# A fused convolution, attention and expert kernel: step places by kind of slot, and all places set anew

## The chip, the cores and the metric

The kernel runs on one core of one Trainium2 chip. The metric is the device time of one execution in microseconds (us), the median over several runs. TensorE is called PE here, VectorE DVE, ScalarE ACT, GpSimd POOL, and SyncE SP. SP issues most of the DMAs. POOL issues the indirect ones (scatters of rows, and adds into the output).

## The reference

The input `x` is 8 images of 56x56 places with 256 channels, in float32, so 25,088 tokens. Cut to what matters:

```python
# layer 0: 32 narrow paths, each 1x1 to 4 channels, 3x3, 1x1 back to 256, with batch norms
paths = vmap(_path)(x, W1, ..., W2, ..., W3, ...)
x = relu(paths.sum(axis=0) + x)
# layer 1, on tokens t of 256 channels
y = _ln_t(t)                                   # attention of 8 heads with 32 channels
kv = einsum('bhnd,bhne->bhde', ln(y), ln(y)) / N          # one matrix for each image
t = t + (einsum('bhnd,bhde->bhne', y, kv) + y)
z = _ln_t(t)                                   # experts: 8, the best 2 for each token
out = z
for e in range(8):
    out = out + combine[:, e:e+1] * (gelu(z @ w1[e] + b1[e]) @ w2[e] + b2[e])
t = t + out
```

Attention needs the sum `kv` over a whole image before it can treat that image's first token, and an expert's tile of rows needs the routing of tokens from many places.

## The kernel before

**Chunks and slots.** An image is cut into 7 chunks of 448 tokens, so there are 56 chunks. The main loop runs over 65 slots. In slot s, the third convolution of chunk s is computed (16 steps of `pair`, two pairs each, and 8 of `sum_paths`), beside the first convolution of chunk s+2, the second one of chunk s+1, the end of chunk s-1 (`end_steps`: transposes, norms per head, and the products that go into `kv`), and the attention of chunk a = s-8. If a is the first chunk of an image, the slot also makes that image's matrix (`image_steps`). From slot 56 on there is no third convolution; this is called the tail here.

**Routing, plans, tiles.** Two chunks at a time are routed (`route_steps`), and their rows scattered by POOL into `regions` by expert. After some chunks (`closing`) a plan of tiles is made (`plan_steps`): which 256 rows of which expert each tile takes. A tile is worked on in five steps (`moe_steps`): `tile_in` (transposes `te`, L1404), two `tile_mid` (products `ph`, L1448, ACT Gelu), and two `tile_out` (products `py`, L1464 and L1468, ACT scaling into `y`), after which POOL adds `y` into the output (L1486). The same steps start the load of later tiles' rows (L1383, 259 KB) and weights (L1393, 513 KB) on SP. There are 210 tiles; slots 19 to 55 have three or four each, and 36 are left after slot 64.

**The order.** PE, DVE and ACT run in the order in which the program emits instructions. The order is not planned: each step has a place between 0 and 1 in its slot, and `issue` sorts the slot's steps by place. The places of `pair` and `sum_paths` follow from weights, and are spread over the slot; those of the other steps come from lists in `places`. A group with a begin and an end (`"tiles"`, `"route"`, `"plan"`) is spread between the two. POOL and SP are not in that order: the framework's scheduler orders them.

**Lists and slots.** Slots 0 to 7 have lists `"... alone"`. The others share one list for each group of steps, with exceptions for the attention of an image's first chunk, for the tail, and for `end_steps` in slots 8 to 20. `"tiles"` holds two begins:

```python
work_of.append((places["tiles"][s <= known_in[r]], places["tiles"][2], moe_steps(upto, goal)))
```

In the first slot in which a new plan is known (`s <= known_in[r]`), tiles begin at the second value, else at the first. These slots are called first slots here: 18, 21, 25, 28, 32, 35, 39, 42, 46, 49, 53, 56 and, in the tail, 59, 60, 62 and 64.

**Kinds of slots.** By a modulo 7, with slots 21 to 55: 0 makes an image's matrix (22, 29, 36, 43, 50); 1 routes one chunk and makes a plan; 2 routes two chunks (24, 31, 38, 45, 52); 3 is a first slot without routing (25, 32, 39, 46, 53); 4 routes two and makes a plan; 5 has no routing (27, 34, 41, 48, 55); 6 is a first slot which routes two (21, 28, 35, 42, 49). So 6 does the work of 2, and 3 nearly that of 5 (5 also scatters the second chunk of the group before).

Of the kernel before, what the change touches and what calls it, by code (L numbers as in the profile page):

```python
# [25 lines left out]
def kernel(  # L26
# [38 lines left out]
    NCH = N // CH  # L65
    NG = P // 32
    NJ = NP // NG
    S = B * NCH
    A = NCH + 1
# [26 lines left out]
    taps = ctx.enter_context(tc.tile_pool(name="taps", bufs=1))  # L96
# [160 lines left out]
    def is_chunk(s):  # L257
        return 0 <= s < S
# [115 lines left out]
    own = setup.tile([P, P // 16, 16], F32, name="own")  # L374
# [229 lines left out]
    def unordered(ins, group, keep=()):  # L604
# [7 lines left out]


    places = {
        "after": [7, 5, 5, 3, 6, 5, 6, 5, 10],
        "attention": [0.108, 0.235, 0.378, 0.514, 0.579, 0.689, 0.744, 0.798, 0.881, 0.94],
        "attention first": [0.396, 0.487, 0.578, 0.669, 0.742, 0.953, 0.99, 0.99, 0.99, 0.99],
        "attention last": [
            0.19, 0.311, 0.432, 0.553, 0.65, 0.65, 0.65,
            0.693, 0.741, 0.778, 0.802, 0.938, 0.938, 0.938,  # L620
        ],
        "attention first last": [
            0.611, 0.692, 0.774, 0.856, 0.921, 0.962, 0.982,
            0.982, 0.982, 0.982, 0.982, 0.982, 0.982, 0.982,
        ],
        "conv1": [0, 0, 0.111],
        "conv1 alone": [0, 0.003, 0.016],
        "conv2": [0.621, 0.658, 0.658, 0.675],
        "conv2 alone": [0.531, 0.629, 0.629, 0.806],
        "end": [0.109, 0.151, 0.244, 0.244, 0.337, 0.431, 0.551, 0.681, 0.761, 0.908],  # L630
        "end first": [0.109, 0.151, 0.244, 0.244, 0.337, 0.431, 0.551, 0.741, 0.771, 0.92],
        "end alone": [0.121, 0.156, 0.166, 0.226, 0.306, 0.386, 0.386, 0.636, 0.73, 0.865],
        "fetch": [0.103],
        "image": [
            0.001, 0.028, 0.054, 0.081, 0.115, 0.134,
            0.161, 0.187, 0.214, 0.241, 0.267, 0.294,
        ],
        "tiles": [0.029, 0.205, 0.99],
        "conv3": [0.7, 0.9],
        "plan": [0.64, 0.983],  # L640
        "route": [0.005, 0.373],
        "route last": [0, 0.002],
        "scatter": [0.302, 0.46],
        "scatter last": [0.35],
        "taps": [0.124],
        "taps alone": [0.413],
    }

    unit, sums = {}, {}
# [916 lines left out]
    def put_off(m):  # L1566

        return m % NCH == NCH - 1 and m + 1 + A < S

    known_in = [  # L1570
        m + A + 1 + (1 if m >= S - NCH else 2) + (1 if put_off(m) else 0) for m in closing
    ]
    r, upto = -1, -2
    waiting, left = [], []
    for s in range(S + A + 1):
        a = s - A
        work_of = []
        era = " alone" if s < A else ""
        if s <= S:
            work_of.append((0.0, 1.0 if is_chunk(s) else 0.1, conv3_steps(s)))  # L1580
        if is_chunk(s + 2):
            work_of.extend(at("conv1" + era, conv1_steps(s + 2)))
        if is_chunk(s + 1):
            work_of.extend(at("taps" + era, [(0.0, lambda: spread_taps(s + 1))]))
            work_of.extend(at("conv2" + era, conv2_steps(s + 1)))
        if is_chunk(s - 1):
            if s < S:
                few = " first" if A <= s < known_in[1] else era
                work_of.extend(at("end" + few, end_steps(s - 1)))
            else:  # L1590
                work_of.append((0.12, 0.99, end_steps(s - 1)))
        if is_chunk(a + 1):
            work_of.extend(at("fetch", [(0.0, lambda: fetch(a + 1))]))
        if is_chunk(a):
            opens = a % NCH == 0
            if opens:
                work_of.extend(at("image", image_steps(a // NCH)))
            if a + A > S:
                work_of.extend(at("attention first last" if opens else "attention last", attn_steps(a)))
            else:  # L1600
                work_of.extend(at("attention first" if opens else "attention", attn_steps(a)))
        work_of.extend(left)
        left = []
        group = waiting
        if waiting and put_off(waiting[0]):
            group = [] if waiting[0] == a - 1 else waiting[:1]
        if group and (len(group) == 2 or group[-1] % NCH == NCH - 1):
            last_image = group[-1] >= S - NCH
            compute, scatters = route_steps(group)
            rt = places["route" if s < S else "route last"]  # L1610
            work_of.append((rt[0], rt[1], compute))
            if last_image:
                work_of.append((places["scatter last"][0], 0.995, sum(scatters, [])))
            else:
                work_of.append((places["scatter"][0], 0.995, scatters[0]))
                left = [(0.0, places["scatter"][1], steps) for steps in scatters[1:]]
            if group[-1] in closing:
                work_of.append((places["plan"][0], places["plan"][1], plan_steps(closing.index(group[-1]))))
            waiting = waiting[len(group) :]
        while r + 1 < len(closing) and known_in[r + 1] <= s:  # L1620
            r += 1
        if r >= 0 and r + 1 < len(closing):
# [3 lines left out]
            work_of.append((places["tiles"][s <= known_in[r]], places["tiles"][2], moe_steps(upto, goal)))  # L1626
# [71 lines left out]
```

## Time and profile before

| what | value |
|---|---|
| median of 3 runs (lowest, highest) | 3053.82 us (3053.51, 3058.21) |
| time of the profiled execution | 3075.17 us |
| span of the profiled execution | 3072.7 us |
| PE busy, matmuls | 2850.7 us, 16901 |
| DVE, ACT, POOL busy | 2143.9, 1923.6, 1801.4 us |
| mean granted PE clock | 0.966 |
| bytes moved by DMA | 538.19 MB |

The profiled execution was 21 us longer than the median run, 0.7%. Busy times are sums of the profile's records; matmuls are pipelined and their ends are modelled, so PE can be called busy while it waits a little. A slot's bounds in the trace are taken from DVE operations on line 669: each of slots 0 to 55 has 32 of them, and a slot is the time from its first to the first of the next.

### The profile page before, as it was taken

To read this page: it belongs to the slowest core of one execution; us is meant where nothing else is said; L and a number is where in the kernel's file an instruction comes from. 1 tells how busy PE (TensorE), PEld (TensorE's weight loads), DVE (VectorE), ACT (ScalarE), POOL (GpSimd) and SP (SyncE) were. 2 spreads that over 40 slices of the span, in tenths; PEclk is the share of its full clock that TensorE was granted. 3 is DMA by queue.
4 is the path that set the end of the run, shared out by engine and by line. 5 is a ranking of instruction groups with operands and counts; after the bars stand their busy time and mean duration, and the time that the engine had idled before them with its cause. 6 is when DMAs were issued, how large, how long until landed. Compare 5 with 4: busy or idle time off the path is not lost.

```text
span 3072.7 us, 54357 instructions
## 1 busy us (share of the span) xinstructions
PE 2850.7 (93%) x16901; PEld 1656.5 (54%) x16901; DVE 2143.9 (70%) x5705; ACT 1923.6 (63%) x3859; POOL 1801.4 (59%) x1333
## 2 busy tenths in 40 slices
PE   7999989899999999999999999999999997887898
PEld 3334444444555555555555555555555554776787
DVE  6777888888878777787777787777778783543100
ACT  4666666556666666666766766666666663444455
POOL 2332254545566765666766766576664555677677
PEclk9999899999999999999999999999999998988899
DMA  3655454447577777777777776788887766998897
GB/s 102 146 118 131 111 149 138 135 111 189 146 180 164 216 168 201 176 182 211 188 193 178 194 205 160 198 193 177 201 171 184 182 172 136 235 246 212 211 225 172
DMA packets 373233, 538.19 MB, mean 175 GB/s; under 512 B 91488, under 2 KB 283344, under 8 KB 372944
## 3 DMA queue, kind: packets, MB, share of 16 engines
q1 hardware_dynamic: 289984, 430.49, 49.9%
q0 software_dynamic: 82368, 103.47, 20.4%
q8 instruction: 135, 2.21, 0.3%
q14 instruction: 154, 1.26, 0.2%
q10 hardware_dynamic: 592, 0.76, 0.1%
HBM read 248.42 MB, written 192.75 MB: 144 GB/s over the span
## 4 chain that ended last, share of the span: by engine, by line
PE 43%; DVE 4%; issue 3%; ACT 3%; POOL 2%; DMA 1%; another core or an unknown queue 1%; POOLq 0%; ACTq 0%; DVEq 0%; SPq 0%
PE ph L1448 10%; PE py L1468 8%; PE c L661 7%; PE su L682 6%; PE te L1404 2%; PE py L1464 2%; PE at L1011 2%; PE c L324 2%; PE kv L838 2%; DVE r L669 1%; ACT r L666 1%; DMA out_dram<-y,index 1%; POOL hsd L802 1%; PE at L1007 1%
## 5 line engine op out<-in xcount | busy, mean ns | idle before, releaser
L669 DVE SCALAR_TENSOR_TENSOR r<-c,nb,r 128x448 f32<-128x448 f32 x1792 | 1126.8, 676 | 370.3 <-ACT r L666 325.2
L666 ACT ACTIVATE r<-c,b3t 128x448 f32<-128x448 f32 x1792 | 1039.0, 635 | 320.0 <-PE c L661 302.4
L661 PE MATMUL c<-hl,W3hl 64*128 64x448 f32 x3584 | 705.8, 428 | 39.9 <-ACT r L666 20.0
L1192 POOL DMA_INDIRECT regions<-pay,rrowi x448 | 429.9, 960 | 290.7 <-PE c L661 162.6
L661 PEld LDWEIGHTS c<-hl,W3hl 64*128 64x128 f32 x3584 | 333.8, 187 | 493.4 <-issue 221.5
L1486 POOL DMA_INDIRECT out_dram<-y,rows x258 | 408.2, 1582 | 323.2 <-ACT y L1472 248.5
L682 PE MATMUL su<-r,gather 128*32 128x448 f32 x3584 | 534.2, 567 | 16.4 <-DVE xT L688 9.2
L1448 PE MATMUL ph<-eT,w 128*128 128x256 f32 x1680 | 460.2, 405 | 35.4 <-ACT hT L1452 13.6
L1472 ACT ACTIVATE y<-py,rows 128x256 f32<-128x256 f32 x420 | 197.4, 474 | 428.3 <-PE py L1468 309.5
L1468 PE MATMUL py<-w,hT 128*128 128x256 f32 x1680 | 432.5, 382 | 1.5 <-issue 1.5
L1448 PEld LDWEIGHTS ph<-eT,w 128*128 128x128 f32 x1680 | 301.8, 196 | 169.1 <-issue 51.7
L802 POOL TENSOR_TENSOR hsd<-hsd,half 112x36 f32<-112x36 f32 x49 | 302.3, 6170 | 101.6 <-DVE hsd L800 101.6
L755 POOL TENSOR_TENSOR norm<-t,hmean 112x512 f32<-112x512 f32 x112 | 115.7, 1060 | 360.7 <-DVE hmean L744 191.6
L1452 ACT ACTIVATE hT<-ph,w 128x256 f32<-128x256 f32 x420 | 198.0, 478 | 196.0 <-PE ph L1448 107.4
L1486 POOL DMA_INDIRECT out_dram<-y,index x162 | 251.1, 1550 | 101.3 <-ACT y L1472 32.7
L1468 PEld LDWEIGHTS py<-w,hT 128*128 128x128 f32 x1680 | 291.3, 191 | 29.2 <-issue 2.3
L682 PEld LDWEIGHTS su<-r,gather 128*32 128x32 f32 x3584 | 99.5, 109 | 199.9 <-issue 98.3
L1464 PE MATMUL py<-b2hl,own 128*128 128x256 f32 x420 | 175.7, 418 | 9.2 <-issue 4.9
L1016 DVE SCALAR_TENSOR_TENSOR X<-at,rs,X 112x256 f32<-112x256 f32 x224 | 106.7, 476 | 105.5 <-PE at L1011 59.3
L324 PE MATMUL c<-R,W2t 96*32 96x448 f32 x1344 | 151.5, 553 | 2.5 <-ACT r L666 2.5
L1464 PEld LDWEIGHTS py<-b2hl,own 128*128 128x128 f32 x420 | 79.9, 190 | 136.7 <-issue 61.5
L1011 PE MATMUL at<-tab,tT 128*112 128x144 f32 x896 | 151.6, 293 | 0.1
(267 smaller groups left out, 3271.7 us busy)
## 6 DMA issues: line engine op xcount, KB each, us to landing
w<-Wd SPq DMA_DIRECT2D x210, 513.0 KB
rows<-regions SPq DMA_DIRECT2D x210, 259.0 KB
xi<-in_x_dram SPq DMA_DIRECT2D x56, 448.0 KB
hl<-hi SPq DMA_DIRECT2D x112, 224.0 KB
tTs<-xT SPq DMA_DIRECT2D x56, 448.0 KB
ts<-t SPq DMA_DIRECT2D x56, 448.0 KB
tT<-tTs SPq DMA_DIRECT2D x56, 448.0 KB
X<-ts SPq DMA_DIRECT2D x56, 448.0 KB
```

Of the source, the lines that this page charges most:

```text
L324: nc.tensor.matmul(ps[0][32 * g : 32 * g + 32, :CH], W2t[:, g, dy, :], R[:, g, :].rearrange("q (r w) -> q r w", w=W58)[:, dy : dy + ROWS, ...
L661: product = nc.tensor.matmul(tiles[g][:, :CH], W3hl[rows, ab, cg, :], hl[rows, ab, :], start=True, stop=True)
L666: nc.scalar.activation(r, tiles[0][:, :CH], AF.Relu, bias=b3t[:, cg, 2 * ab : 2 * ab + 1])
L669: nc.vector.scalar_tensor_tensor(r, tiles[1][:, :CH], nb3[:, cg, 2 * ab + 1 : 2 * ab + 2], r, op0=ALU.max, op1=ALU.add,)
L682: nc.tensor.matmul(ps[32 * c4 : 32 * c4 + 32, :CH], gather, unit.pop((s, 4 * u + c4)), start=(ab == 0), stop=(ab == NQ - 1),)
L802: nc.gpsimd.tensor_tensor(sd, sd, half[:T, :].rearrange("q (k h) -> q k h", k=KT), ALU.pow)
L1011: nc.tensor.matmul(ps[:, f * P : f * P + WT], tT[:, f, k * T : (k + 1) * T], tab[:, f, :], start=False, stop=(f == NF - 1),)
L1192: ins = nc.gpsimd.indirect_dma_start(out=regions[n], out_offset=bass.IndirectOffsetOnAxis(ap=v["row_i"][:, (m - group[0]) * KT + k, n : n ...
L1448: nc.tensor.matmul(ps, w[:, f * C + hf * P : f * C + (hf + 1) * P], eT[:, f, :], start=(f == 0), stop=(f == NF - 1),)
L1464: nc.tensor.matmul(ps, own.to_broadcast([P, P]), b2hl, start=True, stop=False)
L1468: nc.tensor.matmul(ps, hT[:, f, h * P : (h + 1) * P], w[:, (NF + f) * C : (NF + f + 1) * C], start=False, stop=(f == NF - 1),)
L1486: ins = nc.gpsimd.indirect_dma_start(out=out_rows, out_offset=at, in_=y[:, h, :], in_offset=None, compute_op=ALU.add, **partial,).ins
```

## The change

The main loop gets a name for the slot's kind (`era`): `" few"` for slots 8 to 20, `" image"` for slots that make an image's matrix, `" plan"` for those that make a plan; slots 54 and later have none. The lists of attention, both convolutions, taps, end, route and tiles exist once for each kind, and all values were chosen anew.

```diff
     places = {
-        "after": [7, 5, 5, 3, 6, 5, 6, 5, 10],
+        "after": [7, 5, 5, 4, 7, 4, 6, 4, 10],
         "attention": [0.108, 0.235, 0.378, 0.514, 0.579, 0.689, 0.744, 0.798, 0.881, 0.94],
+        "attention few": [0.128, 0.255, 0.398, 0.534, 0.599, 0.709, 0.764, 0.818, 0.901, 0.96],
...
-        "conv2": [0.621, 0.658, 0.658, 0.675],
+        "conv2": [0.621, 0.658, 0.675, 0.675],
+        "conv2 image": [0.556, 0.618, 0.618, 0.635],
+        "conv2 plan": [0.621, 0.658, 0.658, 0.675],
...
-        "end": [0.109, 0.151, 0.244, 0.244, 0.337, 0.431, 0.551, 0.681, 0.761, 0.908],
+        "end": [0.109, 0.151, 0.244, 0.244, 0.337, 0.431, 0.551, 0.681, 0.761, 0.887],
+        "end image": [0.109, 0.201, 0.244, 0.244, 0.337, 0.431, 0.551, 0.686, 0.761, 0.995],
+        "end plan": [0.109, 0.151, 0.244, 0.244, 0.337, 0.431, 0.551, 0.681, 0.761, 0.908],
-        "image": [
-            0.001, 0.028, 0.054, 0.081, 0.115, 0.134,
-            0.161, 0.187, 0.214, 0.241, 0.267, 0.294,
-        ],
-        "tiles": [0.029, 0.205, 0.99],
-        "plan": [0.64, 0.983],
+        "image": [0, 0.023, 0.049, 0.076, 0.085, 0.129, 0.156, 0.182, 0.209, 0.236, 0.247, 0.247],
+        "plan": [0.64, 0.994],
+        "tiles": [0.038, 0.044, 0.986],
+        "tiles image": [0.029, 0.106, 0.99],
+        "tiles plan": [0.029, 0.106, 0.99],
...
-        era = " alone" if s < A else ""
+        few = A <= s < known_in[1]
+        era = " alone" if s < A else " few" if few else " image" if a % NCH == 0 else ""
+        plans = [m + A + (2 if put_off(m) else 1) for m in closing]
+        if not era and s in plans:
+            era = " plan"
+        if s >= S - 2:
+            era = ""
```

The lists of the tail (`"attention last"`, `"attention first last"`) move by some hundredths. `"after"` gives how many tiles slots 56 to 64 take: slots 59 and 60 take one more, 61 and 63 one fewer.

In the order of PE, DVE and ACT this comes to the following. No step is added or dropped. Slots 0 to 7 and the plan slots 23, 26, 37, 44, 47 and 51 keep their order. In first slots 21 to 53, the tiles of the slot begin two or three pair steps earlier and are spread more widely; the order of slot 42 is then that of slot 45, and the order of slot 53 that of slot 48, but for a step here and there that passes its neighbour. In ordinary slots `products` (L838) goes ahead of one `pair` step. In image slots `values` of the first half goes ahead of one `pair` step, `centered` follows `mean` at once, the second convolution comes one `pair` step earlier, and `products` goes to the end of the slot. In slots 9 to 20, `attend` 2 and 3 go behind the next `pair` step. In the tail's first slots, tiles begin ahead of the attention instead of behind its first one or two steps. On POOL, 1086 of 1338 instructions keep their place in the order; where the tail's scatters run, up to four adds go ahead of a burst of them, and the longest run of scatters without an add becomes 11 (it was 14) in slot 56 and 8 (it was 6) in slots 57, 59, 61 and 63.

More of the change, by code (lines that the diff above doesn't have):

```diff
@@ L614 @@
     places = {
-        "after": [7, 5, 5, 3, 6, 5, 6, 5, 10],
+        "after": [7, 5, 5, 4, 7, 4, 6, 4, 10],
         "attention": [0.108, 0.235, 0.378, 0.514, 0.579, 0.689, 0.744, 0.798, 0.881, 0.94],
-        "attention first": [0.396, 0.487, 0.578, 0.669, 0.742, 0.953, 0.99, 0.99, 0.99, 0.99],
+        "attention few": [0.128, 0.255, 0.398, 0.534, 0.599, 0.709, 0.764, 0.818, 0.901, 0.96],
+        "attention first": [0.396, 0.487, 0.578, 0.669, 0.742, 0.953, 0.989, 0.989, 0.989, 0.989],
+        "attention first last": [
+            0.616, 0.697, 0.779, 0.861, 0.921, 0.921, 0.921, 0.939, 0.939, 0.939, 0.939, 0.939,
+            0.939, 0.955,
+        ],
@@ L618 @@
         "attention last": [
-            0.19, 0.311, 0.432, 0.553, 0.65, 0.65, 0.65,
-            0.693, 0.741, 0.778, 0.802, 0.938, 0.938, 0.938,
-        ],
-        "attention first last": [
-            0.611, 0.692, 0.774, 0.856, 0.921, 0.962, 0.982,
-            0.982, 0.982, 0.982, 0.982, 0.982, 0.982, 0.982,
-        ],
+            0.175, 0.296, 0.417, 0.538, 0.635, 0.635, 0.635, 0.678, 0.726, 0.763, 0.787, 0.923,
+            0.923, 0.923,
+        ],
+        "attention plan": [0.108, 0.235, 0.378, 0.514, 0.579, 0.689, 0.744, 0.798, 0.881, 0.94],
@@ L626 @@
         "conv1": [0, 0, 0.111],
-        "conv1 alone": [0, 0.003, 0.016],
-        "conv2": [0.621, 0.658, 0.658, 0.675],
-        "conv2 alone": [0.531, 0.629, 0.629, 0.806],
-        "end": [0.109, 0.151, 0.244, 0.244, 0.337, 0.431, 0.551, 0.681, 0.761, 0.908],
-        "end first": [0.109, 0.151, 0.244, 0.244, 0.337, 0.431, 0.551, 0.741, 0.771, 0.92],
-        "end alone": [0.121, 0.156, 0.166, 0.226, 0.306, 0.386, 0.386, 0.636, 0.73, 0.865],
-        "fetch": [0.103],
-        "image": [
-            0.001, 0.028, 0.054, 0.081, 0.115, 0.134,
-            0.161, 0.187, 0.214, 0.241, 0.267, 0.294,
-        ],
@@ L638 @@
-        "tiles": [0.029, 0.205, 0.99],
-        "conv3": [0.7, 0.9],
-        "plan": [0.64, 0.983],
+        "conv1 alone": [0, 0, 0.014],
+        "conv1 few": [0, 0, 0.111],
+        "conv1 image": [0, 0, 0.111],
+        "conv1 plan": [0, 0, 0.111],
+        "conv2": [0.621, 0.658, 0.675, 0.675],
+        "conv2 alone": [0.531, 0.629, 0.629, 0.806],
+        "conv2 few": [0.621, 0.658, 0.658, 0.675],
+        "conv2 image": [0.556, 0.618, 0.618, 0.635],
+        "conv2 plan": [0.621, 0.658, 0.658, 0.675],
@@ new lines @@
+        "conv3": [0.7, 0.9],
+        "end": [0.109, 0.151, 0.244, 0.244, 0.337, 0.431, 0.551, 0.681, 0.761, 0.887],
+        "end alone": [0.116, 0.151, 0.161, 0.221, 0.301, 0.379, 0.381, 0.631, 0.725, 0.86],
+        "end few": [0.109, 0.148, 0.244, 0.244, 0.337, 0.431, 0.551, 0.741, 0.771, 0.92],
+        "end image": [0.109, 0.201, 0.244, 0.244, 0.337, 0.431, 0.551, 0.686, 0.761, 0.995],
+        "end plan": [0.109, 0.151, 0.244, 0.244, 0.337, 0.431, 0.551, 0.681, 0.761, 0.908],
+        "fetch": [0.103],
@@ L641 @@
+        "image": [0, 0.023, 0.049, 0.076, 0.085, 0.129, 0.156, 0.182, 0.209, 0.236, 0.247, 0.247],
+        "plan": [0.64, 0.994],
         "route": [0.005, 0.373],
+        "route image": [0.005, 0.373],
         "route last": [0, 0.002],
+        "route plan": [0.005, 0.373],
         "scatter": [0.302, 0.46],
@@ L646 @@
         "taps alone": [0.413],
+        "taps few": [0.124],
+        "taps image": [0.114],
+        "taps plan": [0.124],
+        "tiles": [0.038, 0.044, 0.986],
+        "tiles image": [0.029, 0.106, 0.99],
+        "tiles plan": [0.029, 0.106, 0.99],
     }
@@ L1587 @@
             if s < S:
-                few = " first" if A <= s < known_in[1] else era
-                work_of.extend(at("end" + few, end_steps(s - 1)))
+                work_of.extend(at("end" + era, end_steps(s - 1)))
             else:
@@ L1600 @@
             else:
-                work_of.extend(at("attention first" if opens else "attention", attn_steps(a)))
+                name = "attention" + (" first" if opens else era)
+                work_of.extend(at(name, attn_steps(a)))
         work_of.extend(left)
@@ L1609 @@
             compute, scatters = route_steps(group)
-            rt = places["route" if s < S else "route last"]
+            own = era if era in (" plan", " image") else ""
+            rt = places["route" + own if s < S else "route last"]
             work_of.append((rt[0], rt[1], compute))
@@ L1625 @@
                 goal = min(known_after[r] - 2, goal if s < known_in[1] else tiles_by(s))
-            work_of.append((places["tiles"][s <= known_in[r]], places["tiles"][2], moe_steps(upto, goal)))
+            own = era if era in (" plan", " image") else ""
+            mine = places["tiles" + own]
+            work_of.append((mine[s <= known_in[r]], mine[2], moe_steps(upto, goal)))
             upto = goal
```

## Prediction, made before the run

> **What bounds it now.** I read the page's busy times first, then its slices of time.
>
> ```profile
> span 3072.7 us, 54357 instructions
> ...
> PE 2850.7 (93%) x16901; PEld 1656.5 (54%) x16901; DVE 2143.9 (70%) x5705; ACT 1923.6 (63%) x3859; POOL 1801.4 (59%) x1333
> ...
> PE   7999989899999999999999999999999997887898
> ...
> PEclk9999899999999999999999999999999998988899
> ```
>
> PE is the bound, at 93%. 222 us of the span are left idle by it. The middle is full; the dents are in the sixth and eighth slices (384 to 461 and 538 to 614 us, slots 9 to 15, no tiles yet) and from the 34th on (the tail). No step is added or dropped, so what can change is idle time, and time in which PE runs at a low clock.
>
> Next I cut the trace at slot bounds and asked for each engine's busy time by stretch. Columns: bounds, length, then busy time (count) of PE, PEld, DVE, ACT, POOL, then granted clock, DMA share, GB/s.
>
> ```profile
> 309.20:358.30 49.10, 44.33 (x237) 20.89 (x235) 37.35 (x93) 25.50 (x50) 12.52 (x7) 0.83 0.37 96
> ...
> 1151.60:1199.50 47.90, 47.87 (x300) 27.06 (x292) 31.29 (x67) 34.22 (x70) 34.39 (x24) 1.00 0.79 201
> ...
> 1728.60:1773.80 45.20, 44.96 (x278) 25.29 (x278) 31.18 (x66) 31.97 (x65) 32.77 (x23) 1.00 0.75 202
> ...
> 1823.30:1868.20 44.90, 44.68 (x282) 24.43 (x282) 31.29 (x68) 31.91 (x65) 32.23 (x22) 1.00 0.86 209
> 1868.20:1916.30 48.10, 46.15 (x289) 26.21 (x286) 36.95 (x101) 32.11 (x66) 28.59 (x20) 1.00 0.61 164
> ...
> 2017.20:2062.90 45.70, 45.24 (x294) 25.18 (x286) 36.41 (x98) 32.00 (x66) 29.21 (x21) 1.00 0.80 187
> 2062.90:2112.80 49.90, 48.85 (x300) 27.87 (x300) 31.35 (x66) 34.23 (x70) 35.89 (x25) 1.00 0.88 204
> ```
>
> These are slots 8, 27, 39, 41, 42, 45 and 46. Slot 42 (a first slot, three tiles) does the work of slot 45 (three tiles, also routing two chunks), but takes 48.1 us against 45.7; slot 46 (a first slot, four tiles) takes 49.9 against 47.9 of slot 27.
>
> The timeline of PE shows why; behind the arrow stands what ended the idle time in the bracket. In slot 42:
>
> ```profile
> 1872.51 0.46 PE L661 MATMUL c<-hl,W3hl 64*128 64x448 f32 x1 [0.46 <-DVE r L669]
> 1872.90 0.65 PE L729 MATMUL tu<-ident,xT 128*112 128x128 f32 x4
> 1873.48 0.96 PE L682 MATMUL su<-r,gather 128*32 128x448 f32 x8
> 1874.37 0.66 PE L1404 MATMUL te<-ident,rows 128*128 128x128 f32 x4
> ...
> 1879.06 0.22 PE L1146 MATMUL rk<-rboth,earlier 112*112 112x128 bf16 x1 [0.53 <-ACT r L666]
> ```
>
> Until the first `te` there is no tile work, so PE waits for DVE and ACT to free the buffers of `pair`; afterwards three tiles crowd into the rest.
>
> **First slots, the main term.** After the change, the order in slot 42 is that of slot 45, so a first slot should take as long as its ordinary twin has taken. From the stretches:
> - a modulo 7 = 6, three tiles: 47.9, 47.8, 47.8 and 48.1 us (slots 21, 28, 35, 42) against a mean of 46.0 (46.4, 46.0, 45.7 of slots 31, 38, 45): 1.9 x 4 = 7.5. Four tiles: 51.6 (slot 49) against 49.3 (slots 24 and 52, 48.9 and 49.7): 2.3.
> - a modulo 7 = 3, three tiles: 45.8, 45.8, 45.2, 44.9 (slots 25, 32, 39, 53) against 44.7 (44.9, 44.9, 44.3 of slots 34, 41, 48): 1.1 + 1.1 + 0.5 + 0.2 = 2.9. Four tiles: 49.9 (slot 46) against 47.9 (slot 27): 2.0.
>
> Together 14.7 us. The part that is plain idle time of PE (1.95 in slot 42 against 0.46 in slot 45, and so on) is 11.3; I take 14.7 and keep 8 as the low end. Slot 18 only starts loads: nothing. The earlier steps also issue row and weight loads on SP, where a new plan's first load waits for all scatters of its round, with `xi`, `tTs` and the output's base rows queued behind. In slot 42 that load is at 1878.62, and the round's last scatter at 1843.33: 35 us of cover, of which the move takes about 5. Without it, PE would wait by whatever the load is late beyond the two tiles by which rows are loaded ahead.
>
> **Ordinary slots.** `products` passes one `pair` step, 0.68 us of PE (L661 x4 above). Its input is POOL's `scale`. In slots 31, 38 and 45 the first product starts 0.06 us before the second `scale` ends; in slots 10, 12, 14 and 17, where PE waits for it, 0.95 before. So 0.89 us are free: nothing, or up to 0.5 in each of seven slots if POOL is later too. Tiles begin 0.009 of a slot later; such slots leave PE idle for 0.2 to 0.8 us, so over some 20 slots I bound this by -4 and +4. I take +1 for both.
>
> **Plan and image slots.** Plan slots keep their order, but for neighbours: nothing. In image slots DVE runs without pause up to the matrix's last part. Slot 29 shows what PE waits for:
>
> ```profile
> 1254.15 0.46 PE L914 MATMUL cs<-tab,mean_of 128*128 128x128 f32 x2 [0.35 <-issue]
> ...
> 1255.62 0.49 PE L914 MATMUL cs<-tab,mean_of 128*128 128x128 f32 x2 [0.90 <-issue]
> ```
>
> `values` of the first half ahead of two L669 operations (1.27 us together) brings the first `cs` forward, not the second, which waits for all of DVE's queue either way. Their sum stays near 1.25 us: nothing. PE idles 2.7 us in slot 29 (51.4 less 48.7 busy); what is left beside the 1.25 bounds a gain by 1.5, and I take as much for a loss: 7 us either way in five slots.
>
> **Few tiles.** In slot 9, DVE runs without pause from 364.61 to 379.71, and PE waits 0.45 and 0.52 us ahead of `attend` 2 and 3. Which of DVE's operations comes first inside this stretch does not move its end: nothing, and at most 1 us a slot either way, 9 in all.
>
> **Tail.** It has 79 us of PE's idle time (512 less 433 busy, from 2560), most of it beside bursts of scatters:
>
> ```profile
> 2698.52 1.12 PE L1404 MATMUL te<-ident,rows 128*128 128x128 f32 x4 [2.07 <-issue]
> 2702.97 2.08 PE L1448 MATMUL ph<-eT,w 128*128 128x256 f32 x4 [3.33 <-issue]
> 2708.51 2.07 PE L1448 MATMUL ph<-eT,w 128*128 128x256 f32 x4 [3.46 <-issue]
> 2712.76 0.58 PE L1464 MATMUL py<-b2hl,own 128*128 128x256 f32 x1 [2.18 <-issue]
> ```
>
> POOL issues 16 scatters between 2685 and 2711. PE loses 11.0 us in these four waits, and at a clock of 0.79 over 2680 to 2720 another 8.4: 19.4 us for a burst. Slots 56, 61 and 63 show the like. The change mixes adds and scatters anew but takes away none, and no wait there names an add or a place. I take nothing, with one burst, 19.4, as the bound either way.
>
> **The sum.** -14.7 + 1 = -14 us. The profiled execution would go from 3075.2 to 3061, the median from 3053.8 to 3040 (the profile's own time stays 21 us above).
>
> **Rivals.**
> - *No net change*, 3054 us. The twins may be quicker for what the slot before left them: PE's busy time, which is no wait, makes 3.4 of the 14.7. If only half of the 14.7 comes, and ordinary and image slots take +4 and +3 from their bounds, nothing is left. For it: the ordinary slots whose order changes a little were nearly free of waits and can hardly gain. Against: 11.3 us are waits by name. Chance 0.16.
> - *Slower: longer bursts*, 3079 us. The longest run of scatters in slots 57, 59, 61 and 63 goes from 6 to 8. If waits begin only after some 10 us of scatters back to back (in slot 59 they began 11 us into the burst), a longer run makes each burst cost more. Two bursts' worth, 2 x 19.4 = 39, less 14: +25. It decides from one burst's worth on (19.4 - 14 = +5). Against: in slot 56 the run shrinks from 14 to 11, and slot 56's waits (2.70 and 7.33 us) were no worse for 14. Chance 0.12.
> - *Slower: the clock falls in image slots*, 3082 us. Slot 8 has the same waits for `cs`, 0.94 and 0.77 us, and a clock of 0.83 over 49.1 us: 16.7 us at half speed, 8.4 lost. Slots 22 to 50, with 0.35 and 0.90, kept theirs. If the new order adds half a microsecond there, five slots lose 8.4 each: +42 - 14 = +28. Against: DVE does the same work up to the second `cs`. Chance 0.06.
> - *One burst less*, 3021 us, if the adds ahead of the bursts free PE: chance 0.06.
>
> The Trainium skill, page "TensorE: Matmul & The Clock Gate", section "HAM oscillation — how this bites in real kernels", has the rule "no PE-idle gaps >~3.4µs" for keeping the clock. By it the clock rival has no chance, and the sum is 3040 all the same. This trace disagrees: slot 8's clock fell beside gaps of 0.94 us at most.
>
> **The numbers.** Forecast 0.60, no change 0.16, the slower two 0.18, one burst less 0.06. A difference of 0.2%, 6 us, is about what a measurement of this kernel can tell from no change. Faster: 0.60 + 0.06 = 0.66. Range: one burst less at the low end, about 3018; at the upper end +26 from the forecast, 3066, which holds "no change" and the first third of the slower cases.
>
> **Right or wrong.** Right if slots 21, 28, 35 and 42 take about 46.0 us and slot 46 about 47.9, `te` starts before the fourth `pair` step, and the tail from 2552.6 on keeps its 520 us. Wrong if first slots stay near 47.9, if PE's `products` begin to wait for POOL in ordinary slots, or if the tail moves by more than 10 us.

## The result, and the profile after

The changed kernel took 3034.54 us, the median of 6 runs (3028.16 to 3039.70), against 3053.66 (3051.33 to 3059.88, 6 runs) for the kernel before: a ratio of 0.9932, with an interval of 0.9920 to 0.9943. That is 19 us, 0.6%, faster. The forecast was 3040, 14 us faster.

The profiled execution of the changed kernel took 3028.16 us, the lowest of its six runs. The top of its page:

```profile
span 3026.2 us, 54432 instructions
...
PE 2819.3 (93%) x16901; PEld 1649.5 (55%) x16901; DVE 2135.6 (71%) x5705; ACT 1917.8 (63%) x3859; POOL 1800.5 (59%) x1333
...
PE   7999999889999999999999999999999997897898
...
PEclk9999899989999999999999999999999998998999
```

The two profiled executions differ by 47 us, the medians by 19. PE is called busy for 31 us less, though it does the same 16901 matmuls. Part of this is the clock: half of the time at half speed, which is what such a stretch costs, comes to 105.2 us in the profile of before and 87.7 in this one. But slots 21 to 53 lost 1.7 us to the clock in each, and their 9607 matmuls are called busy for 1548.1 us before and 1531.7 after. So delays too small to show as idle gaps can count as busy time. Whoever reads only these two pages would look for 28 us too much. So the first question is which of the two executions is unusual, and the answer changes what the slots of before are worth.

**A second profile of the old order.** One kernel had all step places as before, so the order on every engine was that of before.

> All step places as before the change, so the order of every engine is that of before: a second profile of the same order. Theory 'odd base' (the profiled execution of before, 21 us above its median, was long in places where the order had no part in it): slots 25, 32, 39 take 44.2 to 44.4 us and slot 46 48.8 (45.8, 45.8, 45.2 and 49.9 in the first profile), the tail from slot 56 on 505 to 510 us (520.1), and the time is 3050 to 3058. Rival 'the base was typical': 45.2 to 45.8, 49.9 and 520 again, and the shorter values in the partial kernels came from the changed places.

It took 3054.34 us, just the median. Here are the stretches of time by slot of this second profile (bounds, length, busy time and count of PE, PEld, DVE, ACT and POOL, granted clock, DMA share, GB/s): slots 39, 42, 45, 46, and the tail.

```profile
1725.50:1769.70 44.20, 44.02 (x278) 25.11 (x278) 31.11 (x66) 31.78 (x65) 32.67 (x23) 1.00 0.77 206
...
1864.10:1912.20 48.10, 46.14 (x289) 26.21 (x286) 36.97 (x101) 32.10 (x66) 28.57 (x20) 1.00 0.63 164
2013.10:2058.80 45.70, 45.24 (x294) 25.17 (x286) 36.44 (x98) 32.00 (x66) 29.16 (x21) 1.00 0.81 187
2058.80:2107.60 48.80, 48.39 (x300) 27.67 (x300) 31.27 (x67) 34.35 (x70) 35.86 (x25) 1.00 0.92 208
...
2545.50:3052.00 506.50, 430.51 (x2254) 371.46 (x2253) 144.50 (x685) 237.30 (x549) 363.60 (x266) 0.93 0.88 215
```

Slots 42 and 45 are those of the first profile to 0.1 us. But slot 39 takes 44.2 where it had taken 45.2, slot 46 48.8 where it had taken 49.9, slots 25 and 32 44.3 (45.8 both), and the tail 506.5 where it had taken 520.1. With the same order, the five slots with a modulo 7 = 3 differ by 5.2 us together, and the tail by 13.6: nearly all of the 21 us by which the first profile lay above its median. "Odd base" is right. (The line numbers, as L669 or L754 for the same operation, differ from kernel to kernel, because the lists stand ahead of these lines; the names of the tiles are the same.) Most other slots repeat to 0.1 us from profile to profile, so one profile of an experiment is enough to see what a slot gained, if it is held against this second profile. That is done from here on. Three of the later kernels, run once each, took 3051.19, 3062.36 and 3080.49 us, and the kernel before beside them 3079.19: 14 to 31 us more than the kernels nearest to them, much of it in those same places (tails of 519 to 528 us), so only single slots are read from these three. They and the first profile of before are called the long executions below.

**The changed kernel, slot by slot.** Slots 27, 39, 41, 42, 45 and 46, which answer to those shown of before:

```profile
1140.20:1188.70 48.50, 48.03 (x300) 27.28 (x296) 31.21 (x66) 34.16 (x70) 34.40 (x24) 1.00 0.75 199
1711.30:1754.80 43.50, 43.37 (x278) 24.46 (x274) 30.95 (x66) 31.98 (x65) 32.31 (x23) 1.00 0.94 221
1804.10:1848.60 44.50, 44.28 (x282) 25.09 (x286) 31.08 (x68) 32.17 (x66) 32.27 (x22) 1.00 0.87 210
1848.60:1894.50 45.90, 44.32 (x288) 25.44 (x281) 36.70 (x100) 32.21 (x66) 29.04 (x20) 1.00 0.82 185
1993.80:2040.00 46.20, 45.29 (x294) 25.97 (x290) 36.41 (x98) 32.27 (x66) 29.70 (x21) 1.00 0.77 179
2040.00:2088.60 48.60, 48.14 (x300) 27.28 (x296) 31.24 (x66) 34.15 (x70) 35.42 (x25) 1.00 0.78 215
```

Slot 42 fell from 48.1 to 45.9, as forecast, and slot 39 to 43.5, below the forecast of 44.7. The ordinary slots 27 and 45 grew by 0.5 to 0.6. The timeline of PE in slot 42 (start, length, operation; in the bracket the idle time before and what ended it):

```profile
1847.81 0.66 PE L1418 MATMUL te<-ident,rows 128*128 128x128 f32 x4
...
1865.82 1.13 PE L1462 MATMUL ph<-eT,w 128*128 128x256 f32 x4 [0.73 <-DVE r L683]
...
1887.02 1.83 PE L852 MATMUL kv<-norm 112*128 112x129 f32 x14 [0.43 <-POOL norm L842]
```

`te` now comes 0.8 us ahead of the slot's bound (it came 6.2 us behind it). The waits of `c` and `rk` at its start are gone. A wait of `ph` for DVE and one of `products` (`kv`) for POOL's `scale` are new. The second is the one that the prediction had bounded at 0.5 us a slot for ordinary slots.

Sums over slots, in us, worked out from the profiles (the rest of the columns are the experiments below; "only" means the lists of that kind are new and all others as before):

| slots | before, 2nd profile | after | first only | ordinary only | both | all but first | by slot |
|---|---|---|---|---|---|---|---|
| a mod 7 = 6, first slots (5) | 243.3 | 233.8 | 236.0 | 244.7 | 233.9 | 244.4 | 231.7 |
| a mod 7 = 3, first slots (5) | 226.5 | 223.5 | 227.3 | 228.7 | 224.0 | 228.7 | 223.1 |
| a mod 7 = 2 (5) | 236.1 | 239.7 | 235.9 | 239.9 | 239.8 | 239.3 | 235.9 |
| a mod 7 = 5, to 48 (4) | 181.8 | 181.2 | 181.8 | 181.3 | 181.3 | 181.4 | 180.7 |
| image slots and those behind (10) | 503.6 | 498.8 | 502.6 | 502.1 | 505.3 | 504.1 | 501.0 |
| 8 to 20 | 553.8 | 547.6 | 553.8 | 545.6 | 553.9 | 547.7 | 549.6 |
| 54 and 55 | 98.0 | 95.0 | 98.2 | 97.0 | 98.1 | 94.9 | 95.0 |
| tail | 506.5 | 505.1 | 509.8 | 506.6 | 506.2 | 512.8 | 508.3 |

Before against after, these rows hold 25 of the 26 us between the two profiles: first slots -12.6, a modulo 7 = 2 +3.6, the other ordinary ones -0.6, image pairs -4.8, slots 8 to 20 -6.2, 54 and 55 -3.0, tail -1.4. The first three repeat to about 1 us from profile to profile, the long executions left out; image pairs and slots 8 to 20 also move with the granted clock, in steps of 1.7 us for each 3.4 us at half speed, and the rows above show by how much where the order is the same.

### The profile page after: what moved, and what is told of

It is laid out like the page before. It is cut to its first block, busy times and chain, and to the rows that moved or that the text cites. A ratio compares the mean times of both kernels' runs of the same rounds, so it can differ in the third digit from the quotient of the medians.

```text
span 3026.2 us, 54432 instructions
## 1 busy us (share of the span) xinstructions
PE 2819.3 (93%) x16901; PEld 1649.5 (55%) x16901; DVE 2135.6 (71%) x5705; ACT 1917.8 (63%) x3859; POOL 1800.5 (59%) x1333
## 4 chain that ended last, share of the span: by engine, by line
PE 68%; DVE 11%; ACT 6%; POOL 6%; issue 5%; DMA 3%; SPq 0%; ACTq 0%; POOLq 0%; DVEq 0%
PE c L675 14%; PE su L696 13%; PE ph L1462 10%; PE py L1482 9%; DVE r L683 4%; ACT r L680 4%; PE kv L852 3%; PE at L1025 3%; PE te L1418 3%; PE c L324 3%; POOL hsd L816 3%; PE c L288 2%; PE py L1478 2%; PE tu L743 2%; DMA out_dram<-y,index 2%
## 5 line engine op out<-in xcount | busy, mean ns | idle before, releaser
L675 PE MATMUL c<-hl,W3hl 64*128 64x448 f32 x3584 | 698.2, 428 | 42.2 <-ACT r L680 28.0
L1462 PE MATMUL ph<-eT,w 128*128 128x256 f32 x1680 | 446.9, 397 | 24.1 <-ACT hT L1466 14.7
L1418 PE MATMUL te<-ident,rows 128*128 128x128 f32 x840 | 135.5, 285 | 17.3 <-ACT y L1486 16.9
## 6 DMA issues: line engine op xcount, KB each, us to landing
hl<-hi SPq DMA_DIRECT2D x112, 224.0 KB
```

The source lines that it names most:

```text
L675: product = nc.tensor.matmul(tiles[g][:, :CH], W3hl[rows, ab, cg, :], hl[rows, ab, :], start=True, stop=True)
L1418: nc.tensor.transpose(tp[:, f, h * P : (h + 1) * P], z[:, h, f * P : (f + 1) * P], ident)
L1462: nc.tensor.matmul(ps, w[:, f * C + hf * P : f * C + (hf + 1) * P], eT[:, f, :], start=(f == 0), stop=(f == NF - 1),)
```

## The experiments

**One kind of list at a time.** Four kernels, each with the lists of one kind new.

First slots:

```diff
-        "tiles": [0.029, 0.205, 0.99],
+        "tiles": [0.029, 0.044, 0.99],      # slots 21 to 53
```

> The kernel before, with one number changed: in first slots 21 to 53, tiles begin at 0.044 instead of 0.205. First-slot theory: 12 to 17 us less than before (0.9945 to 0.996 of it), since slots 21, 28, 35 and 42 then take about 46 us (48 before) and slots 25, 32, 39 about 44 (45.5 before), as they do in the two profiles. Tail theory (most of the 19 us came from the new order behind slot 53): no more than 5 us less. Image theory (most came from the slots that make a matrix): no more than 7 us less.

Measured: 3047.17 us, ratio 0.9983 (0.9971 to 0.9995), some 5 us. In the profile the slots with a modulo 7 = 6 fell by 7.4 us together, but those with 3 grew by 0.8. Slots 25 and 42:

```profile
1056.40:1101.20 44.80, 44.36 (x278) 24.52 (x274) 30.94 (x66) 31.88 (x65) 32.90 (x23) 1.00 0.88 220
1861.50:1908.00 46.50, 45.00 (x289) 25.32 (x282) 36.66 (x101) 32.11 (x66) 29.37 (x21) 1.00 0.77 184
```

and the one wait that the timeline of PE shows in slot 25:

```profile
1089.15 1.53 PE L767 MATMUL su<-r,gather 128*32 128x448 f32 x4 [0.44 <-DVE r L754]
```

The early begin takes away the waits at the slot's start, but alone it brings a wait of `sum_paths` (`su`) for DVE late in the slot. Alone, the early begin brings 5 us of run time (2 to 9 by the interval) and 6.5 by these slots, instead of 14.7.

Image slots:

```diff
-        "conv2": [0.621, 0.658, 0.658, 0.675],  "end": [..., 0.151, ..., 0.681, 0.761, 0.908],
+        "conv2 image": [0.556, 0.618, 0.618, 0.635],  "end image": [..., 0.201, ..., 0.686, 0.761, 0.995],
+        "image": [0, 0.023, 0.049, 0.076, 0.085, 0.129, 0.156, 0.182, 0.209, 0.236, 0.247, 0.247],
```

> The kernel before, with the new lists for slots 22, 29, 36, 43 and 50 alone (image, conv2, taps and end there, and the end of the attention of an image's first chunk). First-slot theory, as the prediction has it: nothing, within 7 us. Image theory: by the two profiles, these slots and the ones behind them take 4.8 us less together; if it carries the result, 10 us or more.

Measured: 3049.20 us, 0.9988 (0.9976 to 0.9999). Image slots fell by 1.3 to 2.7 us, and the slots behind them grew by 0.6 to 0.9 (but for slot 30, which lost 1.7 us to the clock in the second profile of before). The five pairs took 6.6 us less together, 4.9 without that clock; the changed kernel's 4.8 has the same loss on both sides. Waits of PE in slot 36 in the second profile of before:

```profile
1586.90 0.49 PE L999 MATMUL cs<-tab,mean_of 128*128 128x128 f32 x2 [0.91 <-DVE tab L992]
1611.09 0.47 PE L746 MATMUL c<-hl,W3hl 64*128 64x448 f32 x1 [0.53 <-ACT r L751]
```

and with image lists alone:

```profile
1585.65 0.49 PE L999 MATMUL cs<-tab,mean_of 128*128 128x128 f32 x2 [0.94 <-DVE tab L992]
```

The wait for `cs` stayed, as the prediction had it. The gain was elsewhere: a wait of `c` at 0.6 of the slot went, and part of what went is `products`, which now runs over the slot's bound.

Tail (`"after"`, the attention lists of the tail, the end of `"plan"`, and the lists of slots 54 and later):

```diff
-        "after": [7, 5, 5, 3, 6, 5, 6, 5, 10],
+        "after": [7, 5, 5, 4, 7, 4, 6, 4, 10],
-        "attention last": [0.19, 0.311, ..., 0.938],
+        "attention last": [0.175, 0.296, ..., 0.923],
```

> The kernel before, with the new values for slots 54 to 64 alone (begin of tiles, attention of the tail, tiles for each slot). First-slot theory, as the prediction has it: nothing, within 10 us. Tail theory: the stretch behind slot 55 is 15.0 us shorter in the profile after, and slots 54 and 55 3.4; if these are no accident of two executions, 15 to 18 us less. Longer-burst rival of the prediction: 5 to 39 us more.

Measured: 3053.72 us, 1.0002 (0.9992 to 1.0013). The tail took 506.1 us in the profile, against 506.5. So the new tail is worth nothing that these profiles can tell: without the long executions, six with the old order there took 506 to 510 us, four with the new one 505 to 513. Slots 54 and 55, though, gave 2.3 us together. The clock has no part in the sum, since the 1.7 us that slot 54 kept were lost in slot 55. PE's longest wait in slot 54 is shorter; first the second profile of before, then this run:

```profile
2486.57 2.29 PE L767 MATMUL su<-r,gather 128*32 128x448 f32 x4 [2.32 <-DVE r L754]
```

```profile
2478.34 0.95 PE L756 MATMUL su<-r,gather 128*32 128x448 f32 x4 [0.75 <-DVE xT L762]
```

All five kernels with these lists took 94.8 to 95.7 us in the two slots, the other nine 97.0 to 98.3. That is too little for the run times to show, whose interval here reaches from 2 us faster to 4 slower.

Slots 8 to 20:

```diff
-        "attention": [0.108, 0.235, 0.378, 0.514, ...],
+        "attention few": [0.128, 0.255, 0.398, 0.534, ...],      # and single steps of end and image
```

> The kernel before, with the new lists for slots 8 to 20 alone. As the prediction has it: nothing, within 9 us. If the difference of the two profiles in these slots is no accident (6.4 us less, nearly all of it in slots 17 and 19, where the low clock of the profile before is missing after): 6 us less.

Measured: 3048.68 us, 0.9990 (0.9980 to 1.0000). The interval touches 1. The profile has 549.1 us for these slots against 553.8, but in the next experiment, which leaves the order of these slots as before, they took 545.6. Between those profiles the granted clock was low for other stretches: the time lost by it, worked out from its records (half of each stretch at half speed), is 41.0 us in the second profile of before and 29.0 in that one. Over all fourteen profiles, eight of the nine with the old order have 553 to 554 us here and that one 545.6, and the five with the new order 543.7 to 549.6: 5.3 us less in the mean, of which 3.1 are clock by the same working. So some gain is likely, up to about 5 us; how much of it the new places bring stays open.

**Ordinary lists alone, with the first slots, and all but the first slots.** The kernel before took 3058.28 us (median of 26 runs) beside these three, 4 us more than the 3054 on which the expectations stand, so the ratios are what to read.

```diff
-        "conv2": [0.621, 0.658, 0.658, 0.675],  "end": [..., 0.761, 0.908],  "tiles": [0.029, 0.205, 0.99],
+        "conv2": [0.621, 0.658, 0.675, 0.675],  "end": [..., 0.761, 0.887],  "tiles": [0.038, 0.205, 0.986],
```

> Only the lists of ordinary slots are new (second convolution's third step and products one pair step later or earlier, tiles begin 0.038 and end 0.986; first slots keep their begin at 0.205). The parts tried so far give -7 (first slots), -5 (image slots), -6 (few tiles) and 0 (tail) in their medians, and the whole change -19. Theory 'the parts add up': -4 to +3 us, 3051 to 3058; slots with a modulo 7 = 2 get 0.3 to 0.6 us longer each, as in the changed kernel, where ph waited for DVE. Theory 'the ordinary lists carry the rest': the first slots with a modulo 7 = 3 fall from 44.3 to 43.5 us with the ordinary lists alone, and the time is 3045 to 3050.

Measured: 3061.22 us, 1.0019 (1.0006 to 1.0032): slower by 6 us, or 2 to 10. Slots with a modulo 7 = 2 got 3.8 us longer together, and the first slots, which still had their late begin, 3.5. Slots 25, 32 and 39 rose to 44.8 instead of falling. In slot 25 `c` waited 0.52 us at 0.58 of the slot:

```profile
1075.39 0.47 PE L746 MATMUL c<-hl,W3hl 64*128 64x448 f32 x1 [0.52 <-ACT r L751]
```

"The ordinary lists carry the rest" is out: by themselves they carry nothing. "The parts add up" had +3 us as its upper end, which the interval just holds; the next run decides about it.

> First slots' begin of tiles (0.044) and the ordinary lists together, all else as before. Theory 'the parts add up': first slots alone gave 3047, so 3043 to 3050; slots 25, 32, 39 stay at 44.3 to 44.8 us. Rival 'the two need each other' (in the changed kernel first slots took 43.5 and 45.9 to 46.05 us, with the early begin alone 44.8 and 46.5): slots 25, 32, 39 at 43.5 and slots 21, 28, 35, 42 at 46.0, and the time 3038 to 3043.

Measured: 3047.87 us, 0.9961 (0.9948 to 0.9973), some 12 us. Slots 25 and 32 took 43.5 us, slots 28, 35 and 42 45.9 to 46.0: "the two need each other". (Slot 39 took 44.1, with a wait of 0.88 us for a DMA.) By the first slots' rows, the begin alone gives -6.5, the ordinary lists alone +3.5, both -11.9: 9 us more than their sum.

```diff
-        "tiles": [0.038, 0.044, 0.986],      # the changed kernel
+        "tiles": [0.038, 0.205, 0.986],
```

> All of the change but the first slots: there tiles begin at 0.205 again. This is the prediction's main term taken out of the changed kernel (3034.5). The prediction's size: +14.7, so about 3049. Theory 'the term is half of that' (first slots alone gave -5 to -7): 3039 to 3043. Rival 'the two need each other': 3045 to 3050, with slots 25, 32, 39 back at 44.3 and slots 21, 28, 35, 42 at 47.9.

Measured: 3053.26 us, 0.9985 (0.9976 to 0.9994). Of 3054 us this ratio makes 3049, which is the prediction's size and inside the rival's range too; the theory of half the term is out. Slots 25, 32 and 39 took 44.8 us, and slots 21, 28, 35 and 42 48.1 to 48.3. Taken out of the changed kernel (0.9932), the early begin is worth 0.53% or 16 us, give or take 4 to 5 by the two intervals; by the first slots' rows 244.4 + 228.7 - 233.8 - 223.5 = 15.8.

**Which of the ordinary values the begin needs.** First slots' begin and the new end of tiles, with `products` and the second convolution as before:

```diff
-        "tiles": [0.029, 0.205, 0.99],
+        "tiles": [0.038, 0.044, 0.986],
```

> First slots' begin at 0.044 and the tiles' new end 0.986, but products and second convolution as before. With the begin alone slots 25, 32, 39 took 44.8 us and waited 0.44 for sum_paths' su at 0.73 of the slot; with all ordinary lists 43.5 and no wait. Between the two orders a tile's mid steps pass sum_paths and products pass a pair step. Theory 'the spread of tiles is what the early begin needs': 43.5 us, su's wait gone, slots 21, 28, 35, 42 at 45.6 to 46.0. Rival 'it is products': 44.8 and the su wait as before.

This is the first of the three kernels of which only single slots are read. Slots 25 and 42, in which the timeline now shows no wait for `su`:

```profile
1056.80:1100.50 43.70, 43.70 (x278) 24.52 (x274) 30.93 (x66) 31.87 (x65) 31.99 (x22) 1.00 0.91 218
1860.30:1905.80 45.50, 44.35 (x288) 25.29 (x280) 36.98 (x101) 32.21 (x66) 28.61 (x20) 1.00 0.81 184
```

The spread is what the begin needs. With the end at 0.986 instead of 0.99, one thing differs in PE's order in slot 25 from the begin alone: a `tile_mid` (four `ph` matmuls) runs ahead of a step of `sum_paths` (eight `su`) instead of behind it, so PE has work while DVE finishes `r`. The wait for `su`, 0.41 to 0.44 us in slots 25, 32 and 39 with the begin alone, is gone in all three. Slots 32 and 39 still took 45.0 and 44.0. In slot 32 this is one wait, at 0.28 of the slot:

```profile
1403.57 0.38 PE L1549 MATMUL py<-b2hl,own 128*128 128x256 f32 x1 [0.88 <-ACT y L1557]
```

The kernel with both parts has the same order on PE, DVE and ACT up to there, but not this wait, and took 43.5 us in slot 32. So this loss is not from the order of these three engines.

**`products` back behind a pair step, in the changed kernel:**

```diff
-        "end": [0.109, 0.151, 0.244, 0.244, 0.337, 0.431, 0.551, 0.681, 0.761, 0.887],
+        "end": [0.109, 0.151, 0.244, 0.244, 0.337, 0.431, 0.551, 0.681, 0.761, 0.908],
```

> The changed kernel with one value back: products of ordinary and first slots at 0.908, behind a pair step, instead of 0.887. In the changed kernel PE waits 0.42 us for kv (products) in slots 31, 38, 45 and in 21, 28, 35, 42. Theory 'products are now too early for POOL's scale' (the prediction's bound for ordinary slots, up to 0.5 each): those waits go, slots 38 and 45 fall from 46.2 to 45.7 and slots 21, 28, 35, 42 from 46.0 to 45.5. Rival 'something else is late in its place': the wait moves to sum_paths or ph, and the slots stay within 0.1 us or grow; slots 25, 32, 39 may leave 43.5.

The wait of `kv` went in all of these slots. Slots 21, 28, 35 and 42 fell by 0.5 each to 45.4 to 45.6. Slots 31, 38 and 45 fell by 0.6, 0.2 and 0.2, but slots 24, 27, 46, 49 and 52, with four tiles, grew by 0.3 each, and 34, 41 and 48 by 0.2. Slots 25, 32 and 39 took 43.7, 44.8 and 44.0, as in the experiment just above, which has the same order there. So `products` were too early where a slot routes two chunks beside three tiles, and not elsewhere.

**Image slots without the late `products`:**

```diff
-        "end image": [0.109, 0.201, 0.244, 0.244, 0.337, 0.431, 0.551, 0.686, 0.761, 0.995],
+        "end image": [0.109, 0.201, 0.244, 0.244, 0.337, 0.431, 0.551, 0.686, 0.761, 0.908],
```

> Only image slots' lists new, with products left at 0.908 there (with 0.995: slots 22, 36, 43 took 50.2, 51.7, 51.7 instead of 51.5, 54.4, 54.4, and the slots behind them 47.6, 47.1, 47.1 instead of 46.7, 46.4, 46.4; -1.9 for a pair of slots). Theory 'the gain is the second convolution's earlier place' (the wait of 0.52 at 0.6 of slot 36 went, and matmuls of pair were shorter): slots 22, 36, 43 between 50.5 and 53, the slots behind at 46.7, 46.4, 46.4, pairs still 1.5 to 2.5 us shorter. Rival 'the gain is products at the end': pairs fall by less than 0.5 us.

Slots 22 and 23 took 98.4 us together (98.2 before, 97.8 with all image lists); slots 36 and 37 took 99.9 (100.9, and 98.8). The late `products` bring all of it in the first pair, and the second half of it in the other, where a wait of `c` went. Neither theory holds for both.

**A version put together slot by slot.** Slots keep the order that was shortest for their kind:

```diff
+        if not era and (a % NCH == 2 or s in (27, 46, 49)):
+            era = " two"        # the lists of before, tiles from 0.029 (first slots 0.044) to 0.99
+        elif not era and a % NCH == 6:
+            era = " six"        # the new lists, products at 0.908
```

> The changed kernel with two more kinds of slots: 24, 31, 38, 45, 52, 27, 46 and 49 take the old ordinary lists (tiles still begin at 0.044 in first slots), and 21, 28, 35, 42 the new ones with products back at 0.908. Slot by slot, from the profiles so far: slots with a modulo 7 = 2 fall from 239.7 us to 235.9 (-3.8), slots 21, 28, 35, 42 from 183.8 to 181.9 (-1.9), 27 from 48.5 to 47.9 (-0.6), 46 and 49 by 0.5 together: -6.8. Theory 'a slot's length follows from its own order': 3026 to 3030 where the changed kernel gives 3034.5, ratio to before 0.990 to 0.992. Rival 'the next slot pays': slots 25, 32, 39 and 53 grow from 43.5 and 44.3 by 0.3 to 0.8 each, and the time stays at 3031 to 3036.

Measured: 3030.47 us (3024.64 to 3032.30, 5 runs), against 3057.03 for the kernel before beside it: 0.9908 (0.9888 to 0.9928). Slots 38, 39, 42, 45 and 46:

```profile
1665.40:1711.10 45.70, 45.26 (x294) 25.47 (x290) 36.47 (x99) 31.99 (x66) 29.17 (x21) 1.00 0.84 187
1711.10:1754.60 43.50, 43.21 (x275) 24.23 (x267) 30.92 (x66) 31.95 (x65) 32.75 (x23) 1.00 0.94 215
1848.60:1894.00 45.40, 44.25 (x288) 25.28 (x280) 36.90 (x100) 32.09 (x66) 28.56 (x20) 1.00 0.82 185
1993.40:2039.20 45.80, 45.29 (x294) 25.49 (x290) 36.41 (x99) 32.02 (x66) 29.18 (x21) 1.00 0.79 187
2039.20:2087.40 48.20, 48.20 (x300) 27.37 (x296) 31.13 (x66) 34.00 (x70) 35.79 (x25) 1.00 0.82 211
```

Every kind fell as worked out (-3.8 us for a modulo 7 = 2, -2.1 for 6, -0.6 for 27 and -0.3 for 46, -6.9 in all), and slots 25, 32, 39 and 53 did not grow: a slot's length followed from its own order. The ratio is lower than the changed kernel's by 0.24%, but the two intervals overlap, so that it beats the changed kernel as a whole is shown by the slots and not by the runs alone.

## Why the prediction was right, step by step

- **Direction and size:** -14 forecast, -19 measured, inside the range. The first slots are the largest part, as forecast. That the sum came so near is partly luck. The two terms that it priced, -14.7 and +1, came to -12.6 and +3.0 in the profiles, so -9.6 together. The rest, 15 us between the two profiles, lies in parts that it put at nothing or did not name: image pairs, slots 8 to 20, 54 and 55, and a little in the tail. (The changed kernel's profile is 6 us below its median, so the run times hold less of this.)
- **Its signs.** Slots 21, 28, 35 and 42 took 45.9 to 46.0 us, as it said. Slot 46 took 48.6 instead of 47.9, and its twin, slot 27, grew to 48.5. That `te` starts before the fourth `pair` step tells nothing: it came after the third one already before the change, and comes after the first now. Two of the three signs of being wrong appeared, too: `products` began to wait for POOL in ordinary slots, and the tail took 15 us less than the first profile's 520, which is no work of the change, since the second profile of the old order had already taken 14 less.
- **First slots, -14.7.** The mechanism is confirmed both ways: with the begin put back the changed kernel loses 16 us. Against the second profile of before, the term is -12.6. Its two halves fared differently. For a modulo 7 = 6, the twins gave -9.8 (7.5 + 2.3), and -9.5 came. For a modulo 7 = 3, -4.9 was forecast and -3.0 came, near it by luck, since two errors mostly cancelled: the bases of 45.8, 45.8, 45.2 and 49.9 were long by 5 us in all by an accident of that execution, and slots 25, 32 and 39 then fell below their twins' 44.7, to 43.5. Why they are quicker than their twins 34 and 41, which took 44.4 and 44.5 after the change, was not looked into. That the order would be "that of slot 45, but for a step here and there" was the step that looked safest. The begin alone gave just -6.5 by the slots, and a step here and there (a `tile_mid` beside `sum_paths`) was worth 1.1 us in slot 25.
- **Ordinary slots, +1 (-4 to +4).** +3.0 by the rows (+3.6 and -0.6). The wait of `products` for POOL came in slots 31, 38 and 45, with 0.42 us each, so the bound of 0.5 was the value to take. "0.89 us are free" is the step that failed. The first product did move forward by 0.7 us, as forecast (from 0.06 us to 0.75 ahead of the end of the second `scale`). But the third product is the one that waits for that `scale`. In the second profile of before, in slot 38, it started 0.27 us behind its end, where 0.06 is the least that slot 10 shows, so 0.2 us were free. Slot 10 already had this wait, 0.51 us, right behind the one that the prediction took for its measure. Slots 24 and 52, with four tiles, grew by 1.2 and 0.9. They took 50.1 and 51.0 where the spread of tiles was new but not `products`, so the spread was the cause there.
- **Image slots, 0 (7 either way).** -4.8 for the pairs, inside the bound. The reading of `cs` was right (0.91 and 0.94 us in slot 36). The step that failed is "what is left beside the 1.25 bounds a gain by 1.5" taken as nothing: the edit to the second convolution and to `products` worked on that rest and on small delays that count as busy. Slot 36 gained 2.7 us, more than its 2.0 us of idle time, though part of it went to slot 37 with `products`.
- **Plan slots, 0:** slots 26, 33, 40 and 47 stayed within 0.2 us. **Slots 8 to 20, 0 (9 either way):** a gain of up to 5 us, cause open, inside the bound.
- **Tail, 0:** -0.4 with its lists alone and -1.4 in the changed kernel's profile. But "keeps its 520 us" was wrong as a number: ten of the fourteen profiles show 505 to 513, the first one of before and the three long ones 519 to 528. Slots 54 and 55 were not in the sum; they gave 3.0 us, 1.7 of it clock.
- **The rivals.** *Longer bursts* and *one burst less*: neither, by the tail. *Clock in image slots*: not decided by the new order. In slot 29 the waits for `c` and `cs` are 0.42 and 1.08 us (below), in sum 0.25 more than before, and 1.7 us were lost to the clock there; but with first and ordinary lists alone, where slot 29 keeps its old order, the same 1.7 were lost, and with image lists alone none. The prediction's "kept theirs" does not hold for slot 50, whose row in the first profile has a clock of 0.97. *No net change* lost by the first slots. In the changed kernel, slot 29:

```profile
1240.49 0.47 PE L675 MATMUL c<-hl,W3hl 64*128 64x448 f32 x2 [0.42 <-ACT h L291]
1242.68 0.49 PE L928 MATMUL cs<-tab,mean_of 128*128 128x128 f32 x2 [1.08 <-DVE tab L921]
```

## What to carry to other kernels

Take a second profile of the kernel before when the first one lies above its median, and compare slot by slot: here most slots repeat to 0.1 us, and those that don't are the ones from which no price should be read. Changes of order do not add up: a begin worth 6.5 us alone and lists that cost 3.5 alone were worth 12 together in the first slots, so test a part by taking it out of the whole as well as by adding it to the old. And a list shared by slots of different load serves one of them: giving each kind the order that was shortest for it brought what the slots said.

## What was not expected of the hardware

**The same order can take longer, with nothing in the program changed.** In the first profile of before, slot 25 has this stretch of PE's timeline:

```profile
1066.77 0.67 PE L661 MATMUL c<-hl,W3hl 64*128 64x448 f32 x3
1068.67 0.46 PE L661 MATMUL c<-hl,W3hl 64*128 64x448 f32 x1 [1.23 <-ACT t L732]
```

In the second profile the same four matmuls run without a break:

```profile
1065.62 0.67 PE L746 MATMUL c<-hl,W3hl 64*128 64x448 f32 x4
```

In the first one, ACT and DVE start again at 1068.0, both released by these matmuls, whose last record ends at 1067.4 (a modelled end); POOL was issuing scatters on both sides of it (0.94 us each, at 1065.8 and 1069.4). The tail, in which the two profiles differ by 13.6 us, is full of scatters too. That scatters are the cause is argued from where the losses lie, and was not tried. In the run of image lists without late `products`, in which slots 25 and 26 have the old order, losses of the same kind cost more (both slots, and then the waits of PE in slot 26):

```profile
1057.60:1105.50 47.90, 46.27 (x278) 26.02 (x278) 31.24 (x66) 32.00 (x65) 32.80 (x23) 0.96 0.74 200
1105.50:1159.40 53.90, 49.76 (x294) 27.59 (x290) 42.49 (x123) 32.07 (x66) 30.95 (x22) 0.94 0.74 161
```

```profile
1141.82 1.53 PE L767 MATMUL su<-r,gather 128*32 128x448 f32 x4 [0.57 <-issue]
1146.71 0.48 PE L746 MATMUL c<-hl,W3hl 64*128 64x448 f32 x2 [1.18 <-issue]
1148.18 0.51 PE L746 MATMUL c<-hl,W3hl 64*128 64x448 f32 x1 [0.99 <-issue]
1149.65 3.78 PE L923 MATMUL kv<-norm 112*128 112x129 f32 x16 [0.96 <-ACT r L751]
```

These two slots took 101.8 us, where they take 91.7 in the second profile of before. The granted clock fell to half for 3.4 us at 1070.0 and for 6.8 us from 1148.5 on, beside waits of 1.23 us and less. The Trainium skill, page "TensorE: Matmul & The Clock Gate", section "HAM oscillation — how this bites in real kernels", has the rule "no PE-idle gaps >~3.4µs" for keeping the clock. This trace disagrees: it shows no gap above 1.23 us in either slot.
